# The last graph of a two-layer graph network: own places for turned h and projected rows, and the second half's tanh and update moved ahead of the previous graph's steps

## The chip, the cores and the metric

The kernel runs on one core of a Trainium2 chip, as one launch for all 64 graphs. The metric is the device time of that core in microseconds (us), the median of repeated runs. Beside it stands one profiled execution, whose span is counted from its first to its last instruction.

## The reference, cut to what matters

Inputs are 64 graphs of 256 nodes with 256 features, `x` (64, 256, 256), and an adjacency `adj` (64, 256, 256). Everything is float32. Layer 0 convolves the features along the nodes, passes messages, and puts both into a gated unit; layer 1 is a graph convolution. Each layer is followed by a layer norm.

```python
# layer 0: x_conv from a 17-tap convolution, x_nmp from message passing
gi = concatenate([x_conv, x_nmp], -1) @ w_ih.T + b_ih
gh = x @ w_hh.T + b_hh
r, z = sigmoid(gi_r + gh_r), sigmoid(gi_z + gh_z)
nn_  = tanh(gi_n + r * gh_n)
x = layernorm(x + (1 - z) * nn_ + z * x)
# layer 1
h    = layer_norm(x, gamma, beta)
conv = (adj @ h) @ W_rel + b_rel + h @ W_root
x = layernorm(x + (x + relu(conv)))
```

The kernel uses that `(adj @ h) @ W_rel` equals `adj @ (h @ W_rel)`, so it projects h first and aggregates after that.

## The kernel before, in words

A graph has 256 nodes; they are handled as two halves of 128 partitions (C = 2), and so are the 256 features. The convolution runs for blocks of eight graphs in a large SBUF buffer, XF, whose operations are sprinkled as small pieces between the steps of the graphs. For each graph k the main loop issues, in an order written out by hand, the gates of k, the messages of k+1 to k+3, and layer 1 of k-1. The order in which the program issues instructions is the order of each engine's own queue; engines wait for each other where one needs the other's data or buffer.

The steps that the change touches, with the lines of the profile:

- `gates_rz` and `gates_n` (L711 to L726) give the sums for r, z and n of one half of a graph: matmuls into a PSUM bank, an addition on VectorE, and for r and z a tanh on ScalarE (a sigmoid by half-angles).
- `update` (L733 to L766) forms tanh of n, the new x, and its statistics; both norms of that point (layer 0's layer norm and the layer norm that opens layer 1) come from one pair of statistics: h for layer 1, and X1 for the residual path. The scales come from GpSimd.
- `transposes_h` (L769) turns h by TensorE so that features lie on partitions; ScalarE copies the result into the tile hT (L777), which has one buffer.
- `project` (L781) multiplies the turned h by W_rel and W_root side by side (L788), eight matmul records for a graph; ScalarE copies the W_rel part into the tile hr (L789), which has one buffer too.
- `aggregate` (L793) multiplies hr by the adjacency into the other half of the same PSUM banks (L800), adds the bias (L802), and yields. Its next steps are relu and residual, statistics and scales (L804 to L813), and then the last norm and the DMA of the output (L816, L817).

The last graph, k = 63, has nothing to overlap with but layer 1 of graph 62. So `last_graph` treats it by halves: `half(n)` is the update of one half in two steps, first the input of tanh and tanh itself (L851 to L853), then the new x, statistics, h and X1 (L855 to L864). `turn_half(n)` turns h of one half (L870, copied by L872), `project_half(n)` projects it (L878, copied by L879), and L903 aggregates. Then each half is normalized and stored (L908 to L915). Steps of graph 62 are put between: `project(62)` after the first turn, `aggregate(62)` after the first half's projection, and the second half's update after that.

`hT` and `hr` of the last graph take the tags of the tiles that the main loop uses, with one buffer each. So the first half's copy into hT waits until `project(62)` has read hT of graph 62, and its copy into hr waits until `aggregate(62)` has read hr of graph 62.

Of the kernel before, what the change touches and what calls it, by code (L numbers as in the profile page):

```python
# [12 lines left out]
F32 = mybir.dt.float32  # L13
# [3 lines left out]
P = 128  # L17
B, N, D = 64, 256, 256
C = D // P
# [56 lines left out]
def gnn_two_layers(  # L76
# [22 lines left out]
    def bank(name):  # L99
        return psum.tile([P, 512], F32, tag="ps", name=name)  # L100

    def stt(o, in0, s, in1, op0=ALU.mult, op1=ALU.add):
        nc.vector.scalar_tensor_tensor(o, in0, s, in1, op0=op0, op1=op1)  # L103
# [133 lines left out]
    XF = const.tile([P, S * D + HP_LEN], F32)  # L237
# [461 lines left out]
    def inputs(k, n):  # L699
        xc, g = XC[k]  # L700
        q = slice(n * P, (n + 1) * P)
        return q, (xc[:, 0, g, q], xc[:, 1, g, q], NMP[k][:, 0, q], NMP[k][:, 1, q])
# [16 lines left out]
    def gates_n(k, n):  # L719
        q, ins = inputs(k, n)  # L720
        pn = bank("ps_n")
        for c in range(C):
            nc.tensor.matmul(pn[:, D:], XT[k][:, c, q], whh[:, c, 2 * D:], start=(c == 0), stop=(c == C - 1))  # L723
        for i, t in enumerate(ins):
            nc.tensor.matmul(pn[:, :D], t, wih[:, i, 2 * D:], start=(i == 0), stop=(i == 3))  # L725
        nc.vector.tensor_add(RZ[k][1][:, n, :], pn, brzn[:, 2 * D:])  # L726

    def stats(mv, k, src):
        st = work.tile([P, 6], F32, tag="bst", name="bst", bufs=4)
        nc.vector.bn_stats(st, src)  # L730
        nc.vector.bn_aggr(mv[:, k, :], st)  # L731
# [37 lines left out]
    def transposes_h(k):  # L769
        hT = work.tile([P, C, N], F32, tag="hT", name="hT", bufs=1)  # L770
        ps = bank("ps_hT")
        for c in range(C):
            for n in range(C):
                q = c * N + n * P
                nc.tensor.transpose(ps[:, q:q + P], H[k][:, n, c * P:(c + 1) * P], ident)
        for c in range(C):
            nc.scalar.activation(hT[:, c, :], ps[:, c * N:(c + 1) * N], AF.Identity,  # L777
                                 bias=gb[:, 1, c:c + 1], scale=gb[:, 0, c:c + 1])
        H[k] = hT
# [13 lines left out]
    def aggregate(k):  # L793

        hr, outs = OUTS[k]
        y = work.tile([P, C, D], F32, tag="y", name="y")
        for n in range(C):
            po = outs[n][:, D:]
            for m in range(C):
                nc.tensor.matmul(po, ADJ[k][:, m, n * P:(n + 1) * P], hr[:, m, :], start=False, stop=(m == C - 1),  # L800
                                 skip_group_check=True)
            nc.vector.tensor_add(y[:, n, :], po, brel)  # L802
        yield
        stt(y, y, 0.0, X1[k], op0=ALU.max, op1=ALU.add)  # L804
        mv = work.tile([P, C, 2], F32, tag="mv", name="mv3", bufs=4)
        for n in range(C):
            stats(mv, n, y[:, n, :])
        q = work.tile([P, C], F32, tag="q3", name="q3", bufs=4)
        sh = work.tile([P, C], F32, tag="sh", name="sh3", bufs=4)
        nc.gpsimd.tensor_scalar(q, mv[:, :, 1], EPS / 4, None, ALU.add)  # L810
        nc.gpsimd.tensor_tensor(q, q, mhalf[:, :C], ALU.pow)
        nc.gpsimd.tensor_mul(sh, mv[:, :, 0], q)
        nc.gpsimd.tensor_scalar(sh, sh, -1.0, None, ALU.mult)  # L813
        yield
        for n in range(C):
            nc.scalar.activation(y[:, n, :], y[:, n, :], AF.Identity, bias=sh[:, n:n + 1], scale=q[:, n:n + 1])  # L816
        nc.scalar.dma_start(out=out[k].rearrange("(c p) d -> p c d", p=P), in_=y)  # L817
        yield


    def step(g):
        if g is not None:
            next(g, None)


    def last_graph(y_before, k):
        nn, w, y = (work.tile([P, C, D], F32, tag=t, name=t, bufs=b) for t, b in (("nn", 1), ("w", 1), ("y", 2)))
        H[k] = work.tile([P, C, D], F32, tag="h", name="h", bufs=1)
        X1[k] = work.tile([P, C, D], F32, tag="x1", name="x1", bufs=2)
        hT = work.tile([P, C, N], F32, tag="hT", name="hT", bufs=1)  # L830
        hr = work.tile([P, C, D], F32, tag="hr", name="hr", bufs=1)
        outs = []

        def scales(mv, columns):

            q = work.tile([P, 2], F32, tag="q", name="qh", bufs=4)
            for i, (f, e) in enumerate(columns):
                nc.gpsimd.tensor_scalar(q[:, i:i + 1], mv[:, 1:2], f, e, ALU.mult, ALU.add)
            nc.gpsimd.tensor_tensor(q[:, :len(columns)], q[:, :len(columns)], mhalf[:, :len(columns)], ALU.pow)
            return q  # L840

        def shift(mv, q):
            sh = work.tile([P, 1], F32, tag="sh", name="shh", bufs=4)
            nc.gpsimd.tensor_mul(sh, mv[:, 0:1], q[:, 0:1])
            nc.gpsimd.tensor_scalar(sh, sh, -1.0, None, ALU.mult)
            return sh

        def half(n):
            rz, gn = RZ[k]
            a, c = nn[:, n, :], w[:, n, :]  # L850
            stt(a, rz[:, n, :D], 1.0, gn[:, n, D:], op0=ALU.add, op1=ALU.mult)  # L851
            stt(a, a, 0.5, gn[:, n, :D])
            nc.scalar.activation(a, a, AF.Tanh)  # L853
            yield
            nc.vector.tensor_sub(c, XG[k][:, n, :], a)  # L855
            stt(c, rz[:, n, D:], 3.0, c, op0=ALU.add, op1=ALU.mult)
            stt(c, a, 4.0, c)
            mv = work.tile([P, 1, 2], F32, tag="mv", name="mvh", bufs=4)
            stats(mv, 0, c)
            mv = mv[:, 0, :]  # L860
            q = scales(mv, [(1.0, 4 * EPS), (1 + EPS, 4 * EPS * EPS)])
            nc.vector.tensor_scalar(H[k][:, n, :], c, mv[:, 0:1], q[:, 1:2], ALU.subtract, ALU.mult)
            sh = shift(mv, q)
            nc.scalar.activation(X1[k][:, n, :], c, AF.Identity, bias=sh, scale=q[:, 0:1])  # L864
            yield

        def turn_half(n):
            ps = bank("ps_hT")
            for c in range(C):
                nc.tensor.transpose(ps[:, c * P:(c + 1) * P], H[k][:, n, c * P:(c + 1) * P], ident)  # L870
            for c in range(C):
                nc.scalar.activation(hT[:, c, n * P:(n + 1) * P], ps[:, c * P:(c + 1) * P], AF.Identity,  # L872
                                     bias=gb[:, 1, c:c + 1], scale=gb[:, 0, c:c + 1])

        def project_half(n):
            ps = bank("ps_out")
            for c in range(C):
                nc.tensor.matmul(ps, hT[:, c, n * P:(n + 1) * P], wrr[:, c, :], start=(c == 0), stop=(c == C - 1))  # L878
            nc.scalar.copy(hr[:, n, :], ps[:, :D])  # L879
            outs.append(ps)  # L880

        halves_ = [half(n) for n in range(C)]
        gates_rz(k, 0)
        gates_n(k, 0)
        step(y_before)
        transposes_h(k - 1)
        step(halves_[0])
        gates_rz(k, 1)
        step(halves_[0])
        gates_n(k, 1)  # L890
        turn_half(0)
        step(halves_[1])
        project(k - 1)
        project_half(0)
        agg = aggregate(k - 1)
        step(agg)
        step(halves_[1])
        turn_half(1)
        step(agg)
        project_half(1)  # L900
        for m in range(C):
            for n in range(C):
                nc.tensor.matmul(outs[n][:, D:], ADJ[k][:, m, n * P:(n + 1) * P], hr[:, m, :], start=False,  # L903
                                 stop=(m == C - 1), skip_group_check=True)
        step(agg)
        for n in range(C):
            o = y[:, n, :]
            nc.vector.tensor_add(o, outs[n][:, D:], brel)  # L908
            stt(o, o, 0.0, X1[k][:, n, :], op0=ALU.max, op1=ALU.add)
            mv = work.tile([P, 1, 2], F32, tag="mv3", name="mvy", bufs=4)  # L910
            stats(mv, 0, o)
            q = scales(mv[:, 0, :], [(1.0, EPS / 4)])
            sh = shift(mv[:, 0, :], q)
            nc.scalar.activation(o, o, AF.Identity, bias=sh, scale=q[:, 0:1])
            (nc.sync, nc.scalar)[n].dma_start(out=out[k, n * P:(n + 1) * P, :], in_=o)  # L915
# [94 lines left out]
    work = ctx.enter_context(tc.tile_pool(name="work", bufs=2))  # L1010
# [17 lines left out]
    for b in range(NB):  # L1028
# [54 lines left out]
        for _ in coming:  # L1083
            pass
    last_graph(y_left, B - 1)


# [41 lines left out]
```

## Time and profile before

| what | value |
|---|---|
| device time, median of 3 runs | 2278.29 us (2275.2 to 2278.82) |
| span of the profiled execution | 2276.3 us, 24486 instructions |
| mean granted TensorE clock | 0.994 |
| stretch from 2200 to 2243 us | TensorE busy 42.97 of 43.00 us, clock 1.00 |
| stretch from 2243 us to the end | TensorE busy 17.14 of 33.30 us, clock 0.82 |

Read the table from the bottom: TensorE is full until the last graph's second half is through its gates, and about half idle after that. The last 33 us hold all that the change moves. In views of single instructions, the number in brackets is the idle time of the engine before the instruction, with the operation that released it.

### The profile page before, as it was taken

What the parts mean: (1) busy time and instruction counts of PE and PEld (TensorE: products, weight loads), DVE (VectorE), ACT (ScalarE), POOL (GpSimd) and SP (SyncE); (2) the same over time, 40 slices, a digit from 0 to 9 for tenths busy, and PEclk for the clock granted to TensorE, in tenths of its full rate; (3) what the DMA queues carried; (4) which work ended last, traced back from release to release, by engine and by line L of the source; (5) the groups of instructions that cost most, each with busy time, mean ns of one, the idle gap of its engine ahead of it and who ended that gap; (6) DMA issues with size and microseconds to landing.
All of it is one profiled execution on the core that took longest, in us unless ns stands there. A gap on an engine that the chain in (4) does not pass through costs nothing.

```text
span 2276.3 us, 24486 instructions
## 1 busy us (share of the span) xinstructions
PE 2224.9 (98%) x8386; PEld 1462.4 (64%) x8386; DVE 1679.6 (74%) x3194; ACT 766.7 (34%) x1588; POOL 470.1 (21%) x935
## 2 busy tenths in 40 slices
PE   8999999999999999999999999999999999999997
PEld 5775666666666676656666666666666566666664
DVE  6966889388883998749896698938889298874444
ACT  6433222532234322443224322343213532243332
POOL 0101222122120321223122121222122022121211
PEclk9999999999999999999999999999999999999998
DMA  5931433214422152223422143221442315321100
GB/s 147 314 112 65 139 102 97 97 47 134 139 75 98 58 166 87 75 102 110 144 75 95 63 138 112 85 101 52 139 134 74 102 37 167 101 79 37 47 23 14
DMA packets 212681, 226.68 MB, mean 100 GB/s; under 512 B 22103, under 2 KB 203854, under 8 KB 212558
## 3 DMA queue, kind: packets, MB, share of 16 engines
q1 hardware_dynamic: 190128, 191.27, 26.6%
q10 hardware_dynamic: 22430, 33.86, 4.3%
q8 instruction: 67, 1.10, 0.2%
q14 instruction: 56, 0.46, 0.1%
HBM read 179.22 MB, written 45.88 MB: 99 GB/s over the span
## 4 chain that ended last, share of the span: by engine, by line
PE 77%; DVE 15%; DMA 2%; issue 2%; POOL 1%; ACT 1%; SPq 0%; ACTq 0%; POOLq 0%; DVEq 0%
PE ps_rz L713 16%; PE ps_k L384 11%; PE ps_rz L711 8%; PE ps_n L725 8%; PE ps_out L788 6%; DVE XF L103 5%; PE ps_c L465 5%; PE ps_nmp L695 4%; PE ps_n L723 4%; PE ps_msg L645 4%; PE ps_out L800 4%; DMA w<-w2m 2%; PE ps_w L229 2%; DVE w L103 1%; DVE bst L730 1%
## 5 line engine op out<-in xcount | busy, mean ns | idle before, releaser
L103 DVE SCALAR_TENSOR_TENSOR XF<-XF 128x512 f32<-128x512 f32 (+2 forms) x800 | 507.9, 666 | 7.4
L752 POOL TENSOR_SCALAR q<-mv 128x2 f32<-128x2 f32 x63 | 31.9, 506 | 1452.7 <-DVE mv L731 1452.7
L384 PE MATMUL ps_k<-w,XF 128*128 128x256 f32 x1316 | 301.9, 385 | 14.9 <-ACT AT L685 11.6
L384 PEld LDWEIGHTS ps_k<-w,XF 128*128 128x128 f32 x1316 | 248.6, 192 | 63.1 <-ACT AT L685 17.3
L726 DVE TENSOR_TENSOR gn<-ps_n,brzn 128x512 f32<-128x512 f32 x128 | 88.1, 688 | 236.8 <-PE ps_n L725 236.8
L717 ACT ACTIVATE rz<-rz 128x512 f32<-128x512 f32 x128 | 80.6, 630 | 509.3 <-DVE rz L716 509.3
L711 PE MATMUL ps_rz<-whh,xT 128*128 128x512 f32 x512 | 240.9, 593 | 0.0
L713 PE MATMUL ps_rz<-wih,xc 128*128 128x512 f32 x512 | 240.6, 592 | 0.0
L713 PE MATMUL ps_rz<-wih,nmp 128*128 128x512 f32 x512 | 240.6, 592 | 0.0
L716 DVE TENSOR_TENSOR rz<-ps_rz,brzn 128x512 f32<-128x512 f32 x128 | 87.2, 681 | 189.5 <-PE ps_rz L713 189.5
L788 PE MATMUL ps_out<-wrr,hT 128*128 128x512 f32 x504 | 226.6, 592 | 0.0
L713 PEld LDWEIGHTS ps_rz<-wih,nmp 128*128 128x128 f32 x512 | 97.3, 190 | 122.5 <-issue 122.5
L713 PEld LDWEIGHTS ps_rz<-wih,xc 128*128 128x128 f32 x512 | 97.3, 190 | 122.4 <-issue 122.2
L788 PEld LDWEIGHTS ps_out<-wrr,hT 128*128 128x128 f32 x504 | 95.7, 190 | 96.2 <-issue 86.3
L656 ACT ACTIVATE msg<-msg 128x512 f32<-128x512 f32 x61 | 38.4, 630 | 334.2 <-DVE msg L654 334.2
L645 PE MATMUL ps_msg<-wms,xT 128*128 128x260 f32 x512 | 131.6, 395 | 4.4 <-DVE XF L400 4.4
L711 PEld LDWEIGHTS ps_rz<-whh,xT 128*128 128x128 f32 x512 | 92.2, 190 | 64.8 <-issue 61.2
L723 PE MATMUL ps_n<-whh,xT 128*128 128x256 f32 x512 | 131.6, 379 | 0.0
L725 PE MATMUL ps_n<-wih,xc 128*128 128x256 f32 x512 | 131.4, 379 | 0.0
L725 PE MATMUL ps_n<-wih,nmp 128*128 128x256 f32 x512 | 131.4, 379 | 0.0
L361 DVE TENSOR_TENSOR XF<-XF 128x512 f32<-128x512 f32 (+3 forms) x128 | 126.1, 1011 | 1.7
L465 PE MATMUL ps_c<-xTc,w 128*128 128x512 f32 x256 | 117.0, 600 | 6.1 <-ACT xTc L457 6.1
(139 smaller groups left out, 3503.0 us busy)
## 6 DMA issues: line engine op xcount, KB each, us to landing
w<-w2m SPq DMA_DIRECT2D x105, 768.0 KB, 6.1
xn<-in_x_dram SPq DMA_DIRECT2D x32, 512.0 KB, 4.4
xt<-xTc ACTq DMA_DIRECT2D x32, 512.0 KB, 3.2
xT<-xt SPq DMA_DIRECT2D x64, 256.0 KB, 3.0
xb<-in_x_dram SPq DMA_DIRECT2D x32, 512.0 KB, 6.0
adj<-in_adjT_dram SPq DMA_DIRECT2D x64, 256.0 KB, 2.8
x<-in_x_dram SPq DMA_DIRECT2D x64, 256.0 KB, 3.0
out_dram<-y ACTq DMA_DIRECT2D x63, 256.0 KB, 2.2
```

What stands on the lines that cost most here:

```text
L103: nc.vector.scalar_tensor_tensor(o, in0, s, in1, op0=op0, op1=op1)
L361: (nc.vector.tensor_add if add else nc.vector.tensor_sub)(sl(o, n), sl(a, n), sl(b, n))
L384: nc.tensor.matmul(ps, X[:, slot, c * P:(c + 1) * P], w(m, c), start=(c == 0), stop=(c == C - 1))
L465: nc.tensor.matmul(pss[o], w1[:, c, o * P:(o + 1) * P], xTc[:, c, :], start=(c == 0), stop=(c == C - 1))
L645: nc.tensor.matmul(ps[:, :D + 4], XT[k][:, c, m * P:(m + 1) * P], wms[:, c, :], start=(c == 0), stop=(c == C - 1 and not idle))
L695: nc.tensor.matmul(ps[:, d * N:(d + 1) * N], MSG[k][:, m, d * P:(d + 1) * P], AT[k][:, m, :], start=(m == 0), stop=(m == C - 1))
L711: nc.tensor.matmul(prz, XT[k][:, c, q], whh[:, c, 0:2 * D], start=(c == 0), stop=False)
L713: nc.tensor.matmul(prz, t, wih[:, i, 0:2 * D], start=False, stop=(i == 3))
L723: nc.tensor.matmul(pn[:, D:], XT[k][:, c, q], whh[:, c, 2 * D:], start=(c == 0), stop=(c == C - 1))
L725: nc.tensor.matmul(pn[:, :D], t, wih[:, i, 2 * D:], start=(i == 0), stop=(i == 3))
L788: nc.tensor.matmul(ps, hT[:, c, n * P:(n + 1) * P], wrr[:, c, :], start=(c == 0), stop=(c == C - 1))
L800: nc.tensor.matmul(po, ADJ[k][:, m, n * P:(n + 1) * P], hr[:, m, :], start=False, stop=(m == C - 1), skip_group_check=True)
```

## The change

The change gives the last graph's hT and hr places in XF, which the convolution has left by then, so that they no longer share a buffer with graph 62. It splits `half(n)` once more, ahead of the write of X1, so that this write can be issued later than h. And it issues the second half's steps earlier: its tanh ahead of the first turn (and so ahead of `project(62)`), its update and turn ahead of `aggregate(62)`, and its write of X1 after its projection. The purpose is that the two halves of graph 63 wait less for graph 62's buffers and queues. No operation is added or removed.

```diff
-        hT = work.tile([P, C, N], F32, tag="hT", name="hT", bufs=1)
-        hr = work.tile([P, C, D], F32, tag="hr", name="hr", bufs=1)
+
+        hT, hr = (XF[:, i * C * D:(i + 1) * C * D].rearrange("p (c n) -> p c n", c=C) for i in range(2))
         outs = []
...
             sh = shift(mv, q)
+            yield
             nc.scalar.activation(X1[k][:, n, :], c, AF.Identity, bias=sh, scale=q[:, 0:1])
             yield
...
         step(halves_[0])
         gates_rz(k, 1)
         step(halves_[0])
+        step(halves_[0])
         gates_n(k, 1)
+        step(halves_[1])
         turn_half(0)
-        step(halves_[1])
         project(k - 1)
         project_half(0)
+        step(halves_[1])
+        turn_half(1)
         agg = aggregate(k - 1)
         step(agg)
+        project_half(1)
         step(halves_[1])
-        turn_half(1)
         step(agg)
-        project_half(1)
         for m in range(C):
```

## The prediction

> **What bounds the kernel now.** I read the busy rows, the slices, and then the end of the program in order of time, because the edit touches `last_graph` alone.
>
> ```profile
> PE 2224.9 (98%) x8386; PEld 1462.4 (64%) x8386; DVE 1679.6 (74%) x3194; ACT 766.7 (34%) x1588; POOL 470.1 (21%) x935
> ...
> PE   8999999999999999999999999999999999999997
> ...
> PEclk9999999999999999999999999999999999999998
> ```
>
> TensorE is busy for 98% of the span: up to the end the kernel is bound by its matmuls, and nothing there changes. Only the last slice (57 us) shows idle time and a lower clock. The stretches of the end show where (columns: stretch, its length, busy us of PE, PEld, DVE, ACT, POOL with their instructions, clock, DMA share, GB/s):
>
> ```profile
> 2245.70:2248.00 2.30, 0.31 (x4) 0.31 (x4) 0.94 (x3) 0.26 (x1) 1.51 (x5) 1.00 0.00 0
> 2248.00:2252.00 4.00, 3.56 (x10) 1.30 (x8) 1.02 (x3) 0.68 (x2) 0.00 (x0) 1.00 0.00 0
> 2252.00:2256.00 4.00, 3.71 (x12) 2.20 (x12) 0.44 (x2) 1.33 (x6) 0.00 (x0) 1.00 0.00 0
> 2256.00:2260.20 4.20, 0.00 (x0) 0.00 (x0) 2.69 (x8) 0.35 (x1) 1.46 (x5) 1.00 0.00 0
> 2260.20:2264.00 3.80, 2.56 (x5) 1.33 (x6) 1.63 (x5) 1.29 (x3) 1.98 (x5) 0.55 0.00 0
> 2264.00:2268.00 4.00, 4.00 (x10) 2.30 (x9) 0.04 (x1) 1.36 (x3) 0.00 (x0) 0.57 0.01 2
> ```
>
> TensorE does nothing from 2256.0 to 2260.2, and after that it runs at 0.55 of its clock until its work is over. The instructions in order of time say why (start, duration, engine, line, what, and in brackets the idle time before with its releaser):
>
> ```profile
> 2248.74 0.42 DVE L103 SCALAR_TENSOR_TENSOR nn<-nn,gn 128x256 f32<-128x256 f32 x1
> 2251.66 0.81 ACT L872 ACTIVATE hT<-ps_hT,gb 128x128 f32<-128x128 f32 x2 [3.32 <-PE ps_out L788]
> 2252.36 0.41 ACT L853 ACTIVATE nn<-nn 128x256 f32<-128x256 f32 x1
> 2256.33 0.41 DVE L855 TENSOR_TENSOR w<-x,nn 128x256 f32<-128x256 f32 x1
> 2259.72 0.41 DVE L862 TENSOR_SCALAR h<-w,mvh,qh 128x256 f32<-128x256 f32 x1 [1.37 <-POOL qh L839]
> 2260.28 0.41 PE L870 MATMUL ps_hT<-ident,h 128*128 128x128 f32 x2 [4.39 <-DVE h L862]
> 2261.84 3.78 PE L878 MATMUL ps_out<-wrr,hT 128*128 128x512 f32 x4 [1.16 <-ACT hT L872]
> 2267.96 0.42 DVE L908 TENSOR_TENSOR y<-ps_out,brel 128x256 f32<-128x256 f32 x1 [6.02 <-PE ps_out L903]
> ```
>
> The second half's tanh (L853) has its input at 2249.16 (first line's end), yet starts at 2252.36: ScalarE's queue is held by the first half's copy into hT (L872), which may not write before `project` of graph 62 has read the one hT buffer (2251.58). Its subtraction L855 then stands in VectorE's queue behind graph 62's two additions L802 (the second starts at 2255.99), so the second h comes at 2260.13. TensorE has run out of other work by then: 4.39 us idle.
>
> **What the Trainium skill says.** "TensorE: Matmul & The Clock Gate", What's actually happening: after an idle window of about 3.4 us the array falls to half its clock, and a busy window of that length brings it back; the windows run freely. The trace agrees: no drop after the 1.99 us of idle before 2247.72, a drop after 4.39 us; L878's records then come 0.86 us apart against 0.43. The same page, Architectural detail, calls ScalarE's and VectorE's queues strictly first in, first out: the trace agrees, as L853 waits behind L872. "SBUF — State Buffer", SBUF: two separate sides: a VectorE operation with two SBUF inputs and a GpSimd operation lock each other out. The trace agrees: GpSimd's L845 took 0.78 us beside the 0.68 us addition into y, 0.23 us otherwise.
>
> **The change part by part.** Times are of the trace before; I play the queues forward.
>
> 1. *hT and hr in XF.* No instruction more or less. XF's last reader, the transposes of L593, ended by 2042.6, so the new place costs no wait. It removes the wait of L872 for `project(62)` and that of L879 for `aggregate(62)`.
>
> 2. *Second half's tanh ahead of the turn.* Now ScalarE's order is x1 of half 0 (2247.74 + 0.60), tanh of half 1, hT of half 0. The tanh starts with its input at 2249.2 and ends at 2249.6 (0.41). hT follows, 0.81, ready at 2250.5. It is queued behind the tanh, but `project_half(0)` only comes up when `project(62)` ends at 2251.58, so this costs nothing; it starts 0.6 us sooner than its 2252.17.
>
> 3. *Second half's update ahead of `aggregate(62)`.* L855 starts at 2249.67 instead of 2256.33. From L855 to the end of h it took 2260.13 - 2256.33 = 3.80 us, with GpSimd's scales inside: h is there at 2253.47, 6.66 us sooner.
>
> 4. *TensorE's new order:* project(62) to 2251.58; project_half(0), 4 x 0.43 = 1.72, to 2253.30; turn_half(1), which needs h plus 0.15 (2260.13 to 2260.28): 2253.62, so 0.32 us idle; 0.41, to 2254.03. Behind it queue `aggregate(62)` (hr of graph 62 was copied by 2252.1), 1.74, to 2255.77, and hT's copy of half 1 (0.81) lies beside that; project_half(1), 1.72, to 2257.49. Final products: the first row of tiles is complete after six of eight records, 6 x 0.215 = 1.29: 2258.78. The copy of hr (2257.55 + 0.37) is there before the fifth record needs it. With 0.08 to VectorE, L908 starts at 2258.86; before: 2267.96. The gap is **9.1 us**. Split up: idle 4.39 becomes 0.32 (4.1); the wait of 0.61 before project_half(0) plus 0.26 inside it (0.9); the wait of 1.16 before project_half(1), hidden by `aggregate(62)` (1.2); and the clock: project_half(1) 3.6 instead of 1.72 and the last products 2.4 instead of 1.29 (together 3.0). These are read at different points and sum to 9.2.
>
> 5. *x1's write of half 1* moves behind hr of half 1 (2257.9 to 2258.6). Its reader, the max of half 1, comes after 2260: nothing.
>
> 6. *What is given back.* Graph 62's own end was hidden in the wait for TensorE; now it comes just ahead. VectorE: second L802 at 2255.85, y 0.69, four statistics 1.2: free at 2258.2, 0.6 us before L908. GpSimd's four (2262.02 to 2263.64, 1.62 us) then run to 2259.9, and up to 0.3 more where VectorE's y locks them out (L839 took 0.85 beside such an operation, 0.58 without one); the first of the last graph comes at 2260.5. ScalarE's two normalizations and the DMA issue (1.09 + 0.38) end near 2261.7, before the first is wanted at 2262.2. So 0 to 0.3; I take 0.1. The tail from L908 to the end stays 2276.3 - 2267.96 = 8.34.
>
> Sum: -9.1 + 0.1 = -9.0, and 2278.3 - 9.0 = **2269.3**.
>
> **The rivals.**
> - *The clock falls all the same.* For it: idle of 1.99 and 0.32 us, with windows that run freely. Against it: 1.99 alone brought no drop, and 5.4 us of dense work follow. If the last project_half and the last products ran at half rate, the 3.0 us of clock come back: 2272.3. A tail that waits for all 1.6 us of graph 62's GpSimd work falls into the same case: 2269.3 + 1.5 = 2270.8.
> - *The tail takes the gain:* the normalizations of 62 and 63 collide on GpSimd, ScalarE and the output queue, and the end stays bound by them. For it: both now fall in 5 us. Against it: the slack under 6. It would leave 2278.
> - *Slower:* `aggregate(62)` used to fill TensorE ahead of the wait, now it is queued behind turn_half(1). If h of half 1 still came at 2260.13 (some wait that I don't see, in ScalarE's or VectorE's queue), its 1.74 us would follow the idle time at half clock, 3.5; with 0.41, 3.45 for project_half(1) and 2.6, L908 comes at 2270.3 instead of 2267.96: 2280.6. Against it: tanh has its input at 2249.16 and nothing is queued ahead of it that waits.
>
> **How the numbers follow.** Forecast 0.72, clock or part of the tail 0.16, tail takes all 0.07, slower 0.05. The limits of 0.2% are 2273.7 and 2282.9. The three runs before lie 3.6 us apart, which is the main width of the forecast: 2267 to 2271.5; the cases at 2271 to 2272.3 with the scatter reach 2273, and with half of the scatter below: 2266.5 to 2273. Faster: nearly all of the forecast and four fifths of the second, 0.85; within 0.2%: the third and parts of the second and fourth, 0.11; slower 0.04.
>
> **What would show it.** In the profile after: tanh of half 1 starting near 2249.2; its subtraction near 2249.7; the idle time before the second turn down from 4.39 to about 0.3; `aggregate(62)` starting behind it and hiding hT's copy; the clock at 1.00 until the last matmul; L908's successor near 2258.9, and 8.3 to 8.6 us from it to the end. The prediction is wrong if the second turn waits over 1 us, if project_half(1) has records 0.86 us apart, or if the tail grows by more than 1 us.

## The result, and the profile after

The changed kernel took 2267.43 us (median of 6 runs, 2264.56 to 2272.86) against 2277.57 us (6 runs, 2275.2 to 2279.92) of the kernel before. The ratio is 0.9959 with a 95% interval of 0.9945 to 0.9974, that is 5.9 to 12.5 us less. In a second comparison of five rounds it was 0.9965 (0.9954 to 0.9977). The forecast was 2269.3.

The profiled execution has a span of 2266.5 us. Of its page, the busy rows and the slices of TensorE and its clock:

```profile
PE 2221.9 (98%) x8386; PEld 1460.8 (64%) x8386; DVE 1678.4 (74%) x3194; ACT 767.3 (34%) x1588; POOL 467.6 (21%) x935
...
PE   8999999999999999999999999999999999999998
...
PEclk9999999999999999999999999999999999999999
```

The instruction counts are the same; only the last slice differs, in both rows. The end in order of time, the same steps that the prediction showed of the kernel before (hT now bears the name XF, and the lines shown that lie after L863 have moved by one to three):

```profile
2247.24 0.42 ACT L853 ACTIVATE nn<-nn 128x256 f32<-128x256 f32 x1 [0.85 <-DVE nn L103]
2247.56 0.79 ACT L873 ACTIVATE XF<-ps_hT,gb 128x128 f32<-128x128 f32 x2
2247.69 0.43 DVE L855 TENSOR_TENSOR w<-x,nn 128x256 f32<-128x256 f32 x1 [0.48 <-ACT nn L853]
2251.08 0.41 DVE L862 TENSOR_SCALAR h<-w,mvh,qh 128x256 f32<-128x256 f32 x1 [1.37 <-POOL qh L839]
2252.86 0.38 PE L871 MATMUL ps_hT<-ident,h 128*128 128x128 f32 x2
2253.08 1.89 PE L800 MATMUL ps_out<-hr,adj 128*128 128x256 f32 x8
2254.80 1.88 PE L879 MATMUL ps_out<-wrr,XF 128*128 128x512 f32 x4
2258.37 0.42 DVE L911 TENSOR_TENSOR y<-ps_out,brel 128x256 f32<-128x256 f32 x1 [0.94 <-PE ps_out L906]
```

The tanh now waits for its own input only, the subtraction for the tanh only, and the second turn for nothing: its line has no bracket. The 4.39 us of idle time are gone.

Absolute times of two executions can't be set side by side here, since the part ahead of the last graph, the same in both kernels, scatters by some us. So from here on all is counted from the start of the first half's h (first L862: 2247.16 before, 2245.20 after). From there to the first addition of the last output (L908, then L911) it was 20.80 us and is 13.17 us; to the end of the span, 29.14 and 21.30. The stretch that the change touches became 7.84 us shorter. The other 1.96 us of the difference between these two spans lie ahead of it: the chance of two executions, not the change.

One thing is not as forecast. `project(62)` (L788) took 5.13 us in the chain of waits instead of 3.45. Stretches of 3.41 us (length, busy PE, PEld, DVE, ACT, POOL, clock, DMA share, GB/s):

```profile
2243.54:2246.95 3.41, 1.42 (x7) 0.74 (x6) 1.87 (x6) 0.60 (x1) 1.51 (x5) 1.00 0.00 0
2246.95:2250.36 3.41, 3.41 (x6) 1.33 (x5) 2.14 (x6) 1.48 (x4) 0.42 (x3) 0.50 0.00 0
2250.36:2253.77 3.41, 3.41 (x13) 1.85 (x12) 0.41 (x1) 1.08 (x4) 1.09 (x3) 1.00 0.00 0
```

For 3.41 us the clock was at half. What came of that is the subject of the experiments.

### The profile page after: what moved, and what is told of

Same layout as the page of the kernel before. It is cut to its first block, busy times and chain, and to the rows that moved or that the text cites. A ratio compares the mean times of both kernels' runs of the same rounds, so it can differ in the third digit from the quotient of the medians.

```text
span 2266.5 us, 24485 instructions
## 1 busy us (share of the span) xinstructions
PE 2221.9 (98%) x8386; PEld 1460.8 (64%) x8386; DVE 1678.4 (74%) x3194; ACT 767.3 (34%) x1588; POOL 467.6 (21%) x935
## 4 chain that ended last, share of the span: by engine, by line
PE 78%; DVE 15%; DMA 2%; issue 2%; POOL 1%; ACT 1%; SPq 0%; ACTq 0%; DVEq 0%; POOLq 0%
PE ps_rz L713 16%; PE ps_k L384 11%; PE ps_rz L711 8%; PE ps_n L725 8%; PE ps_out L788 7%; DVE XF L103 5%; PE ps_c L465 5%; PE ps_nmp L695 4%; PE ps_n L723 4%; PE ps_out L800 4%; PE ps_msg L645 4%; DMA w<-w2m 2%; PE ps_w L229 2%; DVE w L103 1%; DVE bst L730 1%
## 5 line engine op out<-in xcount | busy, mean ns | idle before, releaser
L788 PE MATMUL ps_out<-wrr,hT 128*128 128x512 f32 x504 | 228.3, 596 | 0.0
L788 PEld LDWEIGHTS ps_out<-wrr,hT 128*128 128x128 f32 x504 | 96.3, 191 | 97.3 <-issue 87.5
```

## The experiments

The theory: the order (tanh and update of the second half ahead of graph 62's steps) brings the gain, the places in XF let it go through, and the half clock in `project(62)` is a matter of where TensorE's idle time falls. The rivals: the shared buffers alone were the cause; the place of `aggregate(62)` was; the half clock belongs to the new order.

**Places only.** The old order, with the new places:

```diff
-        hT = work.tile([P, C, N], F32, tag="hT", name="hT", bufs=1)
-        hr = work.tile([P, C, D], F32, tag="hr", name="hr", bufs=1)
+        hT, hr = (XF[:, i * C * D:(i + 1) * C * D].rearrange("p (c n) -> p c n", c=C) for i in range(2))
```

> hT and hr of the last graph in XF, but the order of the kernel before. I count from the start of the first half's h (L862) to the first addition of the last graph's output (20.80 us before, 13.17 after) and to the end of the span (29.14 before, 21.30 after). Theory (it is the order that brings the gain): the second half's tanh starts about 3 us sooner, near 2 us after the first h starts, but the subtraction still stands behind graph 62's two additions on VectorE, so TensorE's idle time before the second turn stays near 4.4 us and the clock still falls: about 20.0 and 28.3, a gain of 0.85 us, from the earlier project_half(0). Rival (the shared buffers were the cause of the late tanh, and the tanh of the late h): a gain of 3 us or more, idle time under 2 us.

In its trace in order of time, the second half's steps and the second turn:

```profile
2247.11 0.42 ACT L853 ACTIVATE nn<-nn 128x256 f32<-128x256 f32 x1 [0.16 <-DVE nn L103]
2254.74 0.42 DVE L802 TENSOR_TENSOR y<-ps_out,brel 128x256 f32<-128x256 f32 x1 [0.51 <-PE ps_out L800]
2255.08 0.41 DVE L855 TENSOR_TENSOR w<-x,nn 128x256 f32<-128x256 f32 x1
2259.02 0.41 PE L870 MATMUL ps_hT<-ident,h 128*128 128x128 f32 x2 [4.39 <-DVE h L862]
```

The tanh is early (2.03 us after the first h starts, against 5.20 before), and nothing comes of it: the subtraction still starts right behind graph 62's second addition, and TensorE is idle for the same 4.39 us. The first addition came at 21.91 us and the end at 30.22, with `project(62)` at half clock, which costs 1.7. The ratio, 0.9985 (0.9977 to 0.9994), says 1.4 to 5.2 us, more than the 0.85 of the theory. So the kernel was measured again, and beside it the kernel before against itself, both on another chip.

> The kernel with the places only once more: its ratio was 0.9985 (0.9977 to 0.9994), 1.4 to 5.3 us, where the end of its trace explains about 0.85 us. Theory (0.85 us is all): the interval holds 0.9996 this time; 20.0 and 28.3 us at full clock in project(62), 21.9 and 30.2 at half clock. Rival (the places bring some 3 us by a way that the end of the trace doesn't show): 0.9985 again with an interval below 0.9996.

> The kernel before against itself, as a measure of what the comparison of two equal kernels gives, and for one more profile of its end. Theory (the scatter of single runs is that of the clock's free-running windows, the same for both): the ratio's interval holds 1. From the start of the first half's h to the first addition of the last graph's output, and to the end: 20.8 and 29.1 us if project(62) runs at full clock; if it runs at half clock, 1.7 us more, 22.5 and 30.8. The half clock comes if [...]the 2.0 us of idle time ahead of the first turn lie in one window. Rival: the ratio's interval leaves 1 out, and then the interval of the kernel with the places only means nothing at this size either.

The places only gave 0.9993 (0.9985 to 1.0001), which holds the theory's 0.9996 and has the 0.9985 at its edge. The two intervals overlap at 1.4 to 3.4 us, and the theory's 0.85 is outside the first, so what the places alone are worth is not settled by the times; shown is that they leave the idle time as it was. The kernel before against itself gave 0.9998 (0.9986 to 1.0009): an interval of this kind is about 0.1% wide to either side, 2.6 us. Gains of 1 us are not to be had from such times, only from the traces. Both profiles missed the expected figures of the end by about a microsecond, in the same way: 20.80 and 29.15 for the places (with `project(62)` at half clock), 19.76 and 28.16 for the kernel before (at full clock). In both the half clock of the very end was over sooner or began later, so that the last products (L903) ran at full clock. So the end of the kernel before is itself not one number.

**Order only.** The changed kernel, with hT and hr in the old tags (the diff above, reversed):

> The order of the changed kernel, but hT and hr of the last graph in the tags of the main loop as before. Same two stretches. Theory: tanh and h of the second half are as early as in the changed kernel (h ends near 6.3 us after the first h starts); hT of half 0 waits for project(62) and hr of half 0 waits for aggregate(62), and hT of half 1 is queued behind that hr on ScalarE, so project_half(1) is not hidden: TensorE idle about 0.6 us before project_half(0) and about 0.9 us before project_half(1). 13.4 at full clock, 15.1 if project(62) runs at half clock as in the changed kernel: 1.7 to 2 us longer than the changed kernel in the same clock. Rival (the places are the larger part): 17 or more.

13.49 us to the first addition and 21.62 to the end, at full clock; ratio 0.9961 (0.9946 to 0.9976). The two waits that the theory named are in the trace with the expected lengths:

```profile
2249.99 1.98 PE L879 MATMUL ps_out<-wrr,hT 128*128 128x512 f32 x4 [0.61 <-ACT hT L873]
...
2254.80 1.98 PE L879 MATMUL ps_out<-wrr,hT 128*128 128x512 f32 x4 [0.88 <-ACT hT L873]
```

So the order carries by far the most of it: 20.80 (or 19.76) to 13.49. The places add 1.51 us, the difference to the 11.98 that the changed kernel has at full clock (below); 1.7 to 2 were expected. The rival of the buffers falls.

**`aggregate(62)` ahead of the second turn in TensorE's queue:**

```diff
         step(halves_[1])
-        turn_half(1)
         agg = aggregate(k - 1)
         step(agg)
+        turn_half(1)
         project_half(1)
```

> The changed kernel with aggregate(62) ahead of the second turn in TensorE's queue (the update is still ahead of it in VectorE's). Same two stretches. Theory: aggregate(62) then covers the wait for h but no longer covers the copy of hT, so TensorE is idle about 0.5 us before project_half(1) and not before the turn: 11.95 at full clock, 13.4 to 13.7 if project(62) runs at half clock; 0.25 to 0.5 longer than the changed kernel in the same clock. Rival (the place of aggregate(62) in TensorE's queue is what brought the gain): 15 or more.

13.98 us, at half clock in `project(62)`, against 13.17 of the changed kernel likewise. TensorE waits where the theory had it:

```profile
2259.99 1.98 PE L879 MATMUL ps_out<-wrr,XF 128*128 128x512 f32 x4 [0.55 <-ACT XF L873]
```

The place of `aggregate(62)` is worth 0.81 us here, more than the 0.25 to 0.5 expected: at half clock TensorE comes to the turn later than h, so that covering the wait for h, which was to offset part of the 0.55, brings nothing. That accounts for 0.55 of the 0.81. Of the rest, 0.16 are the turn, which occupies TensorE for 0.38 us with nothing behind it and for 0.22 in the changed kernel, and 0.10 lie behind the projection's start. This kernel and the next one were timed once each (2273.57 and 2267.76 us), which says nothing at this scatter; only their traces count.

**X1 not deferred** (the added yield and its two steps taken out):

> The changed kernel without the added yield: X1 of each half is written directly after h, so the second half's X1 stands ahead of hT of half 1 in ScalarE's queue. Same two stretches. Theory: X1 waits for GpSimd's shift, about 0.5 us after h, and takes 0.6, so hT of half 1 is 0.5 to 0.7 us later, all of it beside aggregate(62): no difference, 11.7 at full clock or 13.2 with project(62) at half clock. Rival: project_half(1) waits for hT, 0.5 us or more longer.

11.98 us to the first addition, at full clock: no difference, as expected. The end came at 20.36, 0.26 later than in the changed kernel at full clock, and that was not expected. GpSimd's power L839 starts 0.07 us ahead of VectorE's y in the second profile of the changed kernel (first two lines), and together with it here:

```profile
2262.00 0.57 POOL L839 TENSOR_TENSOR qh<-qh,mhalf 128x1 f32<-128x1 f32 x1
2262.07 0.43 DVE L103 SCALAR_TENSOR_TENSOR y<-y,x 128x256 f32<-128x256 f32 x1
...
2259.54 0.43 DVE L103 SCALAR_TENSOR_TENSOR y<-y,x 128x256 f32<-128x256 f32 x1
2259.54 0.85 POOL L839 TENSOR_TENSOR qh<-qh,mhalf 128x1 f32<-128x1 f32 x1
```

The difference goes with the kernel and not with the execution. The same L839 took 0.57 us in all seven profiles of kernels that defer X1, and 0.85 in all five of kernels that do not (the kernel before and the places only, twice each, and this one). VectorE comes to y 0.51 us after its addition starts where X1 is deferred, and 0.44 where it is not; what the 0.07 us are was not tested. So deferring X1 does shorten the end a little, in a way that was not foreseen.

**The half clock.** First the changed kernel again, then with the gap ahead of the first turn filled:

```diff
         step(halves_[1])
+        fill = bank("ps_fill")
+        for _ in range(2):
+            nc.tensor.matmul(fill, ident, brzn[:, :512], start=True, stop=True)
         turn_half(0)
```

> The changed kernel once more. From the start of the first half's h to the first addition of the last graph's output, and to the end of the span: 12.0 and 20.3 us if project(62) runs at full clock, 13.2 and 21.3 if it runs at half clock. So far the half clock came in project(62) in three of six profiles of kernels that all have the same 2.0 us of idle TensorE ahead of the first turn. Theory (the clock's windows run freely, and the idle stretch falls into one of them or not): either value. Rival (the order of instructions decides the clock): 13.2 and 21.3 again.

> The changed kernel with two extra matmuls of 128x512 (1.7 us) into a spare bank, put into TensorE's idle time ahead of the first turn; their sums are not used. Theory (the idle time causes the half clock): idle time ahead of the first turn about 0.3 us, project(62) with records 0.43 us apart, full clock until the last matmul, 12.0 and 20.3 us. Rival (the half clock comes from something else, such as the load before): 13.2 and 21.3 in spite of the filling.

The changed kernel gave 11.98 and 20.10 us this time, at full clock. With the gap filled it was 11.98 and 20.06, also at full clock, and the wait was down to this:

```profile
2245.30 0.41 PE L871 MATMUL ps_hT<-ident,h 128*128 128x128 f32 x2 [0.27 <-DVE h L862]
```

The times show nothing of the filling: ratio 0.9968 (0.9956 to 0.998), beside 0.9965 of the changed kernel in the same comparison. One profile of each could be chance. But the clock's record of every execution shows half clock, while work goes on, in stretches of 3.41 us or two of them, and all these stretches within an execution start on one grid of 3.41 us, from the first to the last. The grid lies elsewhere in each execution. Laid over the 2.0 us of idle time ahead of the first turn (from the end of the gates' matmuls to the turn), it gives:

| kernel | most of the idle time in one window of 3.41 us | project(62) | first addition, us | end, us |
|---|---|---|---|---|
| before | 1.20 | full clock | 20.80 | 29.14 |
| before, again | 1.92 | full | 19.76 | 28.16 |
| places only | 1.98 | half | 21.91 | 30.22 |
| places only, again | 1.99 | half | 20.80 | 29.15 |
| order only | 1.56 | full | 13.49 | 21.62 |
| aggregate ahead | 1.99 | half | 13.98 | 22.12 |
| X1 not deferred | 1.47 | full | 11.98 | 20.36 |
| changed | 1.99 | half | 13.17 | 21.30 |
| changed, again | 1.71 | full | 11.98 | 20.10 |
| changed, gap filled | 0.27 | full | 11.98 | 20.06 |

In these ten profiles `project(62)` ran at half clock where the idle time lay within one window, to 0.01 us, and in no other case; new order and old order are on both sides. The three stretches of the result section are windows of that grid, the idle time in the first, the half clock in the second. The second profile of the changed kernel, on its own grid, shows the other case:

```profile
2244.96:2248.37 3.41, 1.70 (x8) 1.14 (x7) 1.91 (x6) 0.51 (x1) 1.29 (x4) 1.00 0.00 0
2248.37:2251.79 3.42, 3.13 (x9) 1.61 (x10) 2.73 (x7) 1.98 (x5) 0.23 (x1) 1.00 0.00 0
```

The Trainium skill, "TensorE: Matmul & The Clock Gate", What's actually happening, speaks of a whole idle window; for this gap 1.98 us of 3.41 were enough and 1.92 were not. That is no threshold. In the second profile of the kernel before, a later window with 2.01 us of idle time did not bring half clock, and ahead of the last graph much less was enough, as here in the first profile of the changed kernel:

```profile
1096.66:1100.07 3.41, 2.29 (x11) 1.08 (x9) 3.34 (x6) 1.52 (x4) 0.00 (x0) 1.00 0.00 0
1100.07:1103.49 3.42, 3.42 (x9) 2.71 (x10) 3.30 (x6) 0.68 (x2) 0.00 (x0) 0.50 0.00 0
```

Over all whole windows at full clock in the twelve profiles of this document, half clock followed each of the 23 with 2.03 us or more of idle TensorE, and twelve with only 1.12 or 1.13 us. These twelve also hold matmuls with four partitions instead of 128 (L683), as do others of about 1.1 us that were not followed by it. Other windows with 1.5 to 1.9 us idle were mostly not followed by it. So idle time counts but is not all that counts; what else does stays open.

The profile with the gap filled does not test the filling, because its grid has a line at 2244.23. In the changed kernel the gap runs from 1.43 us ahead of the first h's start to 0.56 behind it. Counted so, the gap here would have run from 2243.31 to 2245.30 and been split into 0.92 and 1.07 us even if left open. The first kernel of the next part does test it: its gap, if left open, would have run from 2244.16 to 2246.15, inside the window from 2243.68 to 2247.10. It was filled, and the clock stayed at full, where four of four such gaps left open brought half clock.

**A better version.** If the gap is what it costs, `project(62)` can fill it, as its hT is ready long before. With it, the last products by halves, since TensorE was seen to stop after the first of them:

```diff
         step(halves_[1])
+        project(k - 1)
         turn_half(0)
-        project(k - 1)
-        project_half(0)
         step(halves_[1])
-        turn_half(1)
         agg = aggregate(k - 1)
         step(agg)
+        project_half(0)
+        turn_half(1)
         project_half(1)
...
-        for m in range(C):
-            for n in range(C):
+        for n in range(C):
+            for m in range(C):
                 nc.tensor.matmul(outs[n][:, D:], ADJ[k][:, m, n * P:(n + 1) * P], hr[:, m, :], start=False,
```

The first kernel has the first part, the second both.

> The changed kernel with project(62) ahead of the first turn in TensorE's queue, where it fills the 2.0 us, and aggregate(62) directly behind that turn. Theory: no idle time ahead of project(62), so no half clock; the second turn waits for h as before (6.4 us after the first h starts), hT of half 1 is then uncovered (0.5 us idle), project_half(1) starts 1.0 us sooner than at full clock in the changed kernel: 11.0 and 19.3 us, 1.0 less than the changed kernel at full clock, 2.2 less than at half clock. Rival (nothing but h's chain on VectorE and GpSimd sets the end): 12.0 and 20.3.

> As project(62) ahead of the first turn, and the last products in the order half 0 complete, then half 1 (the loop over halves outside). In the profiles so far TensorE stops after the first of these four matmuls until ScalarE's copy of hr of half 1 is out of the bank that the second one writes. Theory: with half 0's second product second, half 0's sum is ready one matmul (0.43 us) sooner, and the rest of the end follows it, as VectorE takes 1.48 us for each half: 10.55 and 18.9. Rival (the sum of half 1 sets the end): no difference from the kernel with project(62) first.

11.06 and 19.11 us, then 10.58 and 18.68, both at full clock: each step within 0.1 us of what the theory gave for the first addition, and some 0.2 us less for the end. `project(62)` starts without idle time (the first line, of the first kernel), and the first additions came at:

```profile
2244.00 3.60 PE L788 MATMUL ps_out<-wrr,hT 128*128 128x512 f32 x8
2256.65 0.42 DVE L911 TENSOR_TENSOR y<-ps_out,brel 128x256 f32<-128x256 f32 x1 [2.18 <-PE ps_out L906]
...
2256.90 0.42 DVE L911 TENSOR_TENSOR y<-ps_out,brel 128x256 f32<-128x256 f32 x1 [1.69 <-PE ps_out L906]
```

The first h starts at 2245.59 in the first kernel and at 2246.32 in the second. Times: 2266.57 us, ratio 0.9963 (0.9949 to 0.9976), and 2266.99 us, ratio 0.9958 (0.9946 to 0.9970), beside 0.9965 of the changed kernel in the same comparison. By the traces the end of the last version is 1.4 us shorter than that of the changed kernel at full clock and 2.6 shorter than at half; the times can't tell these apart.

## Why the prediction was right, point by point

Counted from the first h's start. "Full" is the second profile of the changed kernel, "half" the first.

| step | forecast | full | half |
|---|---|---|---|
| second h ends | 6.31 | 6.29 | 6.29 |
| project_half(0) starts | 4.42 | 4.24 | 5.94 |
| second turn starts | 6.46 | 6.44 | 7.66 |
| project_half(1) starts | 8.61 | 8.41 | 9.60 |
| first addition | 11.70 | 11.98 | 13.17 |
| end | 20.14 | 20.10 | 21.30 |

- *Steps 1 to 3, tanh and update:* held within 0.02 us, in every kernel with the new order. XF costs no wait.
- *Step 4, TensorE's order:* the idle time before the second turn was 0.32 us at full clock, as forecast; at half clock TensorE came later than h and it was zero, which gave back part of what the clock took. `aggregate(62)` covered hT's copy. Two terms were mis-sized, with opposite signs. A turn occupies TensorE for 0.24 us, not 0.41 (the span of its records), which makes project_half(1) start 0.2 sooner. And the last products took 3.57 us from the start of project_half(1) to the first addition, not 3.09: I let the copy of hr run beside the first four records, but TensorE stops after two, with a wait in its weight loads:

```profile
2257.15 1.16 PEld L906 LDWEIGHTS ps_out<-XF,adj 128*128 128x128 f32 x6 [0.43 <-ACT XF L880]
```

  The third record writes the bank of half 1, from whose other part ScalarE is still copying hr. The Trainium skill, "PSUM — Partial Sum Buffer", PSUM bank collisions raise a hardware error, asks for guarding by bank and not by address; the program's waits follow that, with 0.43 us here. That the last version gained 0.48 us by putting half 0's second product into this place agrees with it.
- *Step 5:* X1's move is worth nothing up to the first addition, as said; shown by the kernel without it. The 0.26 us that it is worth behind that were not foreseen.
- *Step 6:* nothing was given back. The tail from the first addition was 8.13 and 8.12 us against 8.34; graph 62's last GpSimd operation took 0.45 instead of 0.23 us, but was done before the last graph's scales were wanted. The 0.2 less is L839's 0.57 instead of 0.85, which goes with X1's move. That the end at full clock, 20.10, meets the forecast's 20.14 so closely is luck in the sizes: 0.28 us too little up to the first addition, 0.32 too much behind it.
- *The rival of the clock* was mis-placed. I took the one profile of the kernel before, with no drop after 1.99 us of idle time, as evidence against it, together with 5.4 us of dense work, which are 5.2 by the forecast's own times (2253.62 to 2258.78). It is a matter of the grid: four of the nine profiles with that gap had the half clock after it. It struck `project(62)`, not the last products, so that the expected sign, clock at 1.00 until the last matmul, failed in the first profile and held in the second. Of the 1.70 us that it took there, 1.19 reached the first addition, because TensorE then no longer waited for h, which is 0.48 us from start to start at full clock (2.20 between the starts of project_half(0) and the turn, less 1.72 of records). The "clock 3.0 us" of the old end, which I counted as a fixed part of the gain, is 2.0 by the same count in the kernel before's second profile, where the half clock lay elsewhere.
- *The tail and the slower case* did not occur.

## What to carry to other kernels

When a stage ends the program, write down for each engine what stands ahead of the instruction that the end waits for: an early tanh alone left TensorE's idle time as it was, because the next step stood behind another graph's additions on another engine; moving the whole chain made the end seven to nine microseconds shorter. Fill TensorE's gaps of 2 us with work that is ready, as they can cost more than their length. Where runs scatter by 0.1% or more from a cause outside the change, measure the change in the trace, from a mark just ahead of it.

## What the runs showed of the hardware that was not expected

- The half clock comes on a grid of 3.41 us that is fixed within an execution and lies elsewhere in the next. The 2.0 us of idle time ahead of the first turn brought it when they lay within one window (four of four profiles), and not when at most 1.92 of them did (five of five). Windows with 1.12 us of idle time brought it elsewhere, so idle time is not the whole measure.
- The same grid goes with the scatter between runs. Ahead of the last graph the profile before has four half-clock windows and the profile after three, and each can cost up to 1.7 us where TensorE is the bound. Over the twelve profiles (two of them from another chip) the first half's h starts at 2245.2 us on average with two such windows ahead of it, at 2246.2 with three, at 2247.6 with four, and at 2249.7 in the one with five. With three alone it still varies by 4.4 us, so they are not all of the scatter.
- A difference of 0.07 us in the start of VectorE's y goes with 0.28 us in GpSimd's L839 beside it: 0.57 where L839 started ahead of y, 0.85 where both started together, in all twelve profiles. VectorE's own operation took 0.42 to 0.43 us in all of them: these traces show GpSimd held up by VectorE, not the mutual lock that the prediction read into them.
